# A bilinear block's contraction operands: one copy in DRAM, five replica slots and three product slots

## The chip, the cores and the metric

The kernel runs on one core of a Trainium2 chip. The metric is the device time of a whole launch in microseconds (us). The core has a matrix engine (TensorE, PE in the profile, with its weight loads as PEld), three engines for element-wise work (VectorE or DVE, ScalarE or ACT, GpSimd or POOL), SyncE (SP), which here only issues transfers, and sixteen DMA engines that all the queues share.

## The reference

The input is 16 images of 56 x 56 pixels with 128 channels in float32. Four blocks follow each other, each with a residual and a group normalization ahead of it: window attention, a triangle product, a Fourier operator, and a bilinear block. The change is in the last, which is, cut to what matters:

```python
xp = jax.nn.silu(x @ W1) @ W2                     # 160 channels: q (8 x 16), k (16), v (16)
q, k, v = ...                                     # each normalized over its 16 channels
K_H1 = conv(k, H1_w) + P1                         # per pixel 16 x 16
kernel = jnp.einsum('xnk,xkd->xnd', q, K_H1)      # contraction 1
feature = conv(v, H2_w)                           # per pixel 16 x 16
V_G = conv(v, G_w) + I                            # per pixel 16 x 16
feature = jnp.einsum('xvw,xvd->xwd', V_G, feature)
out = jnp.einsum('xnd,xvd->xvn', kernel, feature)
```

The convolutions are 3 x 7, one filter per pair of channels. The kernel regroups the last two contractions: kernel is contracted with the convolved features first (contraction 2), and the result with V_G (contraction 3). Every one of the three contracts, for each pixel, 8 rows of 16 numbers with a 16 x 16 matrix.

## The kernel before, in words

An image stays on chip as 128 channels x 3136 pixels. Images take one of two lanes in turn, and each lane has its own large scratch tile (the arena), its own small tiles, PSUM tiles and DRAM tiles, so two images are in work at a time. The program is traced image by image, block by block; what each engine gets, and in which order, is then laid out by the tile framework's planner, which plays the program forward with its own estimates of time (`schedule_with_timeline_sim=True`). The order on each engine and on each queue is fixed at build time: an engine or a queue whose next instruction waits does nothing else in the meantime.

The bilinear block (`_bilinear`) goes over an image in seven chunks of 448 pixels. `project` (L1291) makes the normalized input, the silu and the second product; its q part, 128 channels x 448 pixels in PSUM, goes to `kept`. Its k and v part is normalized and written to a zero-padded plane in DRAM (L1338, ScalarE's queue); `spread` (L1347, SyncE's queue) reads that back shifted by seven columns, which makes a convolution a matmul (`conv`, L1362 to L1369).

`kept` (L1284 to L1289) copies 128 x 448 numbers from PSUM to SBUF on ScalarE (L1287) and writes them to a tile in DRAM (L1288, ScalarE's queue; the tile is called dy in the profile). The DRAM tile is 128 x 3584: each row is written eight times side by side. `contract` (L1372) reads it back so that the 128 partitions hold 16 numbers, each for eight columns of the matrix: four reads of 448 KB each (L1381, SyncE's queue), each of two groups i, to a slot of `reps`, of which there are three. A product on VectorE (L1384) multiplies a replica with the matrix's two halves into a slot of `prods`, of which there are four. After two products (n = 0, then n = 1) TensorE sums them with a constant matrix in 16 matmuls of 32 columns (`together`, L364 and L367: the first goes ahead and the others are queued behind it). A contraction thus has four reads, four products and two groups of matmuls. Chunk by chunk there are three contractions, the first two of which end in `kept`, as the projection does: 3 x 7 x 16 = 336 writes, 1344 reads and 1344 products. The main loop takes, in one turn, contraction 3 of chunk q - 2, the projection of chunk q + 2, contraction 2 of chunk q - 1 and contraction 1 of chunk q.

All slots are reused in turn: a read waits until the product that last used its replica slot has ended, and a product until the matmuls that last read its product slot have ended. The arena has room for 9856 columns of both: 3 x 896 + 4 x 1792.

Of the kernel before, what the change touches and what calls it, by code (L numbers as in the profile page):

```python
# [36 lines left out]
F32 = mybir.dt.float32  # L37
# [5 lines left out]
P = 128  # L43
# [4 lines left out]
CH = 448  # L48
# [255 lines left out]
def tile_blocks(ctx: ExitStack, tc: tile.TileContext, ins, out, at, stages=(0, 1, 2, 3)):  # L304
    nc = tc.nc
# [5 lines left out]
    def pool(name, bufs, **kw):  # L311
        return ctx.enter_context(tc.tile_pool(name=name, bufs=bufs, **kw))
# [5 lines left out]
    dyp = [pool(f"dy{k}", 8, space=bass.MemoryType.DRAM) for k in range(2)]  # L318
# [5 lines left out]
    lane = [0]  # L324
    count = [0]

    def uid(s):
        count[0] += 1
        return f"{s}{count[0]}"
# [14 lines left out]
        return ps2[lane[0]].tile([P, 2, 512], F32, tag="ps2", name=uid("psd"))  # L344

    def dram():
        return dyp[lane[0]].tile([P, 8 * CH], F32, tag="dy", name=uid("dy"))

    def bc(ap, axis, n):

# [896 lines left out]
def _bilinear(env):  # L1247
    e = _Env(env)
    nc, mm, tt, ts, act, C, W, bc = e.nc, e.mm, e.tt, e.ts, e.act, e.C, e.W, e.bc
    reduce = nc.vector.tensor_reduce  # L1250
    NH, D = 8, 16
# [12 lines left out]
    def planes(t, start, dims):  # L1264

        return bass.AP(tensor=t.tensor, offset=t.offset + start, ap=[list(d) for d in dims])

    def run(b, xt):
        nm, rs = e.group_norm(xt)
        ar = e.arena()  # L1270
# [5 lines left out]
        staged = [ar[96:P, k * SPAN : (k + 1) * SPAN] for k in range(2)]  # L1276
        nc.gpsimd.memset(ar[96:P, 0 : 2 * SPAN], 0.0)
        zs = [ar[:, 3968 + k * 896 : 4864 + k * 896] for k in range(3)]
        reps = [ar[:, 6656 + k * 896 : 7552 + k * 896] for k in range(3)]
        prods = [ar[:, 9344 + k * 1792 : 11136 + k * 1792] for k in range(4)]  # L1280
        norms = ar[:TT, 16512:16792]
        count = [0, 0, 0]

        def kept(p):  # L1284

            t, d = e.w2(), e.dram()
            nc.scalar.copy(t[:, :CH], p[:, :CH])  # L1287
            nc.scalar.dma_start(out=d.rearrange("p (k t) -> p k t", k=8), in_=bc(t[:, :CH], 1, 8))  # L1288
            return d  # L1289

        def project(q):  # L1291
# [9 lines left out]
            mm(p[:, :CH], lhsT=W("l3w2a")[:, :P], rhs=ha[:, :CH], start=True, stop=False)  # L1301
            mm(p[:, :CH], lhsT=W("l3w2b")[:, :P], rhs=hb[:32, :CH], start=False, stop=True)
            dq = kept(p)
            sq = e.w2()
            act(sq[:, :CH], p[:, :CH], AF.Square)
# [66 lines left out]
        def contract(y, z):  # L1372

            acc = e.psb()
            yv = y.rearrange("(i n a) (k t) -> n (a k) i t", n=2, a=D, k=8)
            for n in range(2):
                done = []
                for two in (0, 2):
                    rep = reps[count[1] % 3].rearrange("p (i t) -> p i t", i=2)
                    count[1] += 1  # L1380
                    nc.sync.dma_start(out=rep, in_=yv[n][:, two : two + 2, :])  # L1381
                    t4 = prods[count[2] % 4].rearrange("p (i h t) -> p i h t", i=2, h=2)
                    count[2] += 1
                    tt(t4, bc(rep, 2, 2), bc(z, 1, 2), ALU.mult)  # L1384
                    done += [t4[:, 0], t4[:, 1]]
                e.together(
                    dict(
                        out=acc[32 * i : 32 * i + 32, :CH],
                        lhsT=C("red")[:, (2 * n + h) * 32 : (2 * n + h + 1) * 32],
                        rhs=done[i][:, h],  # L1390
                        start=n == 0 and h == 0,
                        stop=n == 1 and h == 1,
                    )
                    for h in range(2)
                    for i in (3, 0, 1, 2)
                )
            return acc

        def last(q, y, z):
            acc = contract(y, z)  # L1400
            y = e.w2()
            nc.scalar.copy(y[:, :CH], acc[:, :CH])
            p = e.psb()
            for a in range(4):
                nc.tensor.transpose(p[:TT, a * P : (a + 1) * P], y[:, a * TT : (a + 1) * TT], C("ident"))
            o = e.w2()
            tt(
                o[:TT, :].rearrange("p (a w n) -> p a n w", a=4, n=NH),
                p[:TT, :].rearrange("p (a n w) -> p a n w", a=4, n=NH),
                bc(norms[:, q * 40 : (q + 1) * 40].rearrange("p (a g) -> p a g", g=10)[:, :, :NH], 3, D),  # L1410
                ALU.mult,
            )
            p = e.psb()
            for a in range(4):
                c0 = q * CH + a * TT
                nc.tensor.transpose(p[:TT, a * P : (a + 1) * P], xt[:, c0 : c0 + TT], C("ident"))
            tt(o[:TT, :], p[:TT, :], o[:TT, :], ALU.add)
            nc.sync.dma_start(
                out=e.of[b, q * CH : (q + 1) * CH, :].rearrange("(a p) c -> p a c", p=TT),
                in_=o[:TT, :].rearrange("p (a c) -> p a c", a=4),  # L1420
            )
# [3 lines left out]
        for q in range(NCH + 2):  # L1425
            if 0 <= q - 2:
                last(q - 2, *feat.pop(q - 2))
            if q + 2 < NCH:
                queries[q + 2] = project(q + 2)
            if 0 <= q - 1 < NCH:  # L1430
                zf, zg = conv("l3wf", 1), conv("l3wg", 1)
            if q < NCH:
                spread(1, q)
            if 0 <= q - 1 < NCH:
                feat[q - 1] = kept(contract(kern.pop(q - 1), zf)), zg
            if q < NCH:
                zk = conv("l3wk", 0)
                if q + 1 < NCH:
                    spread(0, q + 1)
                kern[q] = kept(contract(queries.pop(q), zk))  # L1440
# [26 lines left out]
```

## Time and profile before

| what | value |
|---|---|
| median of 5 runs | 14956.74 us (14919.47 to 15004.44) |
| the profiled execution, and its span | 14989.26 us; 14987.2 us |
| granted TensorE clock, mean | 0.781 |
| PE, DVE, ACT, POOL busy | 78%, 63%, 25%, 9% |
| PE weight loads busy | 43% |
| moved by DMA | 2106.93 MB, mean 141 GB/s |
| q1 (SyncE's queue) | 560,000 packets, 823.94 MB, 17.7% of sixteen engines |
| q10 (ScalarE's queue) | 365,712 packets, 639.44 MB, 12.1% |
| q0 (GpSimd's queue, the Fourier block's table reads) | 165,120 packets, 629.61 MB, 15.7% |
| replica writes (dy<-w, L1288) | 336, of 1792 KB each |
| replica reads (arena<-dy, L1381) | 1344, of 448 KB each |
| products (L1384) | 1344, mean 2018 ns |
| a copy of `kept` on ScalarE (L1287) | 336, mean 532 ns |

The profile is of one execution. A row of its cost groups has the line, the engine, the operation, what it writes and reads, how often, the busy time in us, the mean of one in ns, and the idle time of the engine just ahead of it, with what ended most of that. Lines L364 and L367 are helpers, shared by several blocks; the contraction's matmuls there are those with psb<-arena,cst and 128*32. Time that an engine's queue spends waiting is counted for the queue (SPq is SyncE's). KB of a transfer are those that the instruction moves.

### The profile page before, as it was taken

What the parts mean: (1) busy time and instruction counts of PE and PEld (TensorE: products, weight loads), DVE (VectorE), ACT (ScalarE), POOL (GpSimd) and SP (SyncE); (2) the same over time, 40 slices, a digit from 0 to 9 for tenths busy, and PEclk for the clock granted to TensorE, in tenths of its full rate; (3) what the DMA queues carried; (4) which work ended last, traced back from release to release, by engine and by line L of the source; (5) the groups of instructions that cost most, each with busy time, mean ns of one, the idle gap of its engine ahead of it and who ended that gap; (6) DMA issues with size and microseconds to landing.
All of it is one profiled execution on the core that took longest, in us unless ns stands there. A gap on an engine that the chain in (4) does not pass through costs nothing. (4 is left out here: it accounts for less than half of the span.)

```text
span 14987.2 us, 218307 instructions
## 1 busy us (share of the span) xinstructions
PE 11644.3 (78%) x91360; PEld 6410.9 (43%) x91360; DVE 9494.1 (63%) x13537; ACT 3724.7 (25%) x6236; POOL 1326.9 (9%) x2554
## 2 busy tenths in 40 slices
PE   7788687876888778877778777887778877778665
PEld 5454354533544334533345344453434534345342
DVE  6765766667665666656675666747667575665645
ACT  3222231222322223212223122231322313223111
POOL 0120001100011000110010100201002010020010
PEclk9877888778877788777886778868787777886767
DMA  1336704475045751274631736418264272642636
GB/s 31 99 113 229 259 5 117 129 258 192 11 111 166 235 177 40 72 216 154 215 90 40 224 120 209 127 46 241 95 207 112 75 226 83 210 107 77 203 88 217
DMA packets 1091813, 2106.93 MB, mean 141 GB/s; under 512 B 98320, under 2 KB 974096, under 8 KB 1089680
## 3 DMA queue, kind: packets, MB, share of 16 engines
q1 hardware_dynamic: 560000, 823.94, 17.7%
q0 software_dynamic: 165120, 629.61, 15.7%
q10 hardware_dynamic: 365712, 639.44, 12.1%
q8 instruction: 722, 11.83, 0.3%
q14 instruction: 259, 2.12, 0.0%
HBM read 1412.72 MB, written 667.03 MB: 139 GB/s over the span
## 5 line engine op out<-in xcount | busy, mean ns | idle before, releaser
L1384 DVE TENSOR_TENSOR arena<-arena 128x1792 f32<-128x1792 f32 x1344 | 2669.8, 2018 | 1285.9 <-DMA arena<-dy 997.8
L364 PE MATMUL psb<-arena,cst 128*32 128x448 f32 (+1 forms) x1728 | 1111.6, 735 | 1205.8 <-DVE arena L1384 1103.4
L367 PE MATMUL psb<-arena,cst 128*32 128x448 f32 (+1 forms) x10368 | 2031.9, 705 | 1.8 <-ACT arena L995 1.7
L1173 DVE TENSOR_TENSOR arena<-arena 112x1344 f32<-112x1344 f32 x1024 | 1569.2, 1554 | 453.9 <-DMA arena<-table 429.6
L367 PE MATMUL psd<-arena 112*64 112x224 f32 (+1 forms) x6144 | 1477.8, 472 | 0.0
L1171 POOL DMA_DIRECT2D arena<-table x2048 | 1055.2, 518 | 3726.0 <-PE psd L367 1002.5
L364 PE MATMUL psd<-arena 112*64 112x448 f32 x2048 | 1130.2, 639 | 99.0 <-DVE arena L1173 94.3
L364 PEld LDWEIGHTS psb<-arena,cst 128*32 128x32 f32 (+1 forms) x1728 | 205.2, 155 | 1603.9 <-DVE arena L1384 1084.8
L367 PEld LDWEIGHTS psd<-arena 112*64 112x64 f32 x6144 | 619.1, 156 | 591.5 <-issue 580.4
L367 PEld LDWEIGHTS psb<-arena,cst 128*32 128x32 f32 (+1 forms) x10368 | 580.2, 143 | 650.8 <-issue 578.7
L662 PE MATMUL psd<-wgt,arena 128*64 128x128 f32 x7168 | 582.4, 313 | 120.7 <-DVE arena L674 93.4
L1067 DVE TENSOR_TENSOR arena<-w,coef 128x1792 f32<-128x1792 f32 x256 | 507.4, 2020 | 195.4 <-PE psb L367 184.3
L662 PEld LDWEIGHTS psd<-wgt,arena 128*64 128x64 f32 x7168 | 493.2, 157 | 297.6 <-issue 219.6
L1369 ACT COPY arena<-psd 128x896 f32<-128x896 f32 x336 | 304.4, 906 | 1238.7 <-DVE arena L1384 843.3
L887 PEld LDWEIGHTS psb<-cst,arena 128*64 128x64 f32 x10752 | 509.5, 198 | 145.4 <-issue 70.3
L887 PE MATMUL psb<-cst,arena 128*64 128x32 f32 (+1 forms) x10752 | 526.1, 272 | 57.8 <-ACT arena L853 40.9
L367 PE MATMUL psd<-arena,wgt 85*32 85x448 f32 x2688 | 511.3, 635 | 24.8 <-DMA arena<-padded 24.7
L367 PE MATMUL psb<-arena 128*64 128x448 f32 x1792 | 511.4, 648 | 0.0
L1287 ACT COPY w<-psb 128x448 f32<-128x448 f32 x336 | 178.8, 532 | 1337.6 <-PE psb L367 1046.7
L364 PE MATMUL psd<-arena,wgt 85*32 85x448 f32 x896 | 453.6, 629 | 64.9 <-DMA arena<-padded 43.8
L585 PE MATMUL psb<-cst,arena 128*49 128x128 f32 x2048 | 357.6, 329 | 167.5 <-DVE arena L580 56.4
L1196 PE MATMUL psb<-cst,w 128*112 128x56 f32 x1024 | 185.9, 347 | 329.1 <-DVE w L1193 328.1
(290 smaller groups left out, 19435.4 us busy)
## 6 DMA issues: line engine op xcount, KB each, us to landing
arena<-table POOLq DMA_DIRECT2D x2048, 294.0 KB, 9.2
dy<-w ACTq DMA_DIRECT2D x336, 1792.0 KB
arena<-dy SPq DMA_DIRECT2D x1344, 448.0 KB
arena<-padded SPq DMA_DIRECT2D x896, 162.8 KB
w<-x SPq DMA_DIRECT2D x112, 224.0 KB
out<-w SPq DMA_DIRECT2D x112, 224.0 KB
padded<-arena ACTq DMA_DIRECT2D x336, 62.0 KB
arena<-arena POOLq DMA_DIRECT2D x16, 784.0 KB, 10.4
```

The source lines that it names most:

```text
L364: done = mm(**first)
L367: mm(**kw)
L585: nc.tensor.transpose(p[:WIN, i * P : (i + 1) * P], s3[:, 4 * g + i, :], C("ident"))
L662: mm(p[half : half + 64, i // 4, i % 4 * P : (i % 4 + 1) * P], lhsT=xh[:, c0 : c0 + 64], rhs=W(w).rearrange("p (k c) -> p k c", c=64)[:, : ...
L887: mm(p[64 * c : 64 * c + 64, i * nl : (i + 1) * nl], lhsT=src[:, t * T : t * T + 64], rhs=fc[:, c], start=True, stop=True)
L1067: tt(t4, bc(ys[c][:, l0 : l0 + 4, :], 1, 8), bc(coef[:, c, h0 : h0 + 8, l0 : l0 + 4], 3, T), ALU.mult,)
L1171: nc.gpsimd.dma_start(out=t[hh * T : (hh + 1) * T, :], in_=bc(tflat[q, two, hh], 0, T))
L1173: tt(t4, bc(x3[:, :, s], 1, 2), t4, ALU.mult)
L1196: mm(p[:TT, l * T : (l + 1) * T], lhsT=o[:, l * TT : (l + 1) * TT], rhs=C("unpair"), start=True, stop=True)
L1287: nc.scalar.copy(t[:, :CH], p[:, :CH])
L1369: nc.scalar.copy(z, p[:, :, :CH])
L1384: tt(t4, bc(rep, 2, 2), bc(z, 1, 2), ALU.mult)
```

## The change

The DRAM tile shrinks from 128 x 3584 to 128 x 448, and `kept` writes each row once. The 128 rows stand in SBUF in the order (i, n, a) with i of 4, n of 2 and a of 16; in DRAM they are now ordered (n, a, i), so that the groups i of one (n, a) lie side by side. `contract`'s read takes two neighbouring groups as one run of 896 numbers and repeats it for eight partitions, by a step of 0 in the source; before, it read two runs of 448 for each partition, each from its own copy. The bytes that land in SBUF are the same. The replica slots become five and the product slots three; the columns that both take in the arena stay 9856 (5 x 896 + 3 x 1792).

```diff
     def dram():
-        return dyp[lane[0]].tile([P, 8 * CH], F32, tag="dy", name=uid("dy"))
+        return dyp[lane[0]].tile([P, CH], F32, tag="dy", name=uid("dy"))
...
-        reps = [ar[:, 6656 + k * 896 : 7552 + k * 896] for k in range(3)]
-        prods = [ar[:, 9344 + k * 1792 : 11136 + k * 1792] for k in range(4)]
+        reps = [ar[:, 6656 + k * 896 : 7552 + k * 896] for k in range(5)]
+        prods = [ar[:, 11136 + k * 1792 : 12928 + k * 1792] for k in range(3)]
...
             nc.scalar.copy(t[:, :CH], p[:, :CH])
-            nc.scalar.dma_start(out=d.rearrange("p (k t) -> p k t", k=8), in_=bc(t[:, :CH], 1, 8))
+            nc.scalar.dma_start(out=planes(d, 0, ((CH, 4), (4 * CH, 32), (1, CH))), in_=t[:, :CH])
             return d
...
             acc = e.psb()
-            yv = y.rearrange("(i n a) (k t) -> n (a k) i t", n=2, a=D, k=8)
             for n in range(2):
                 done = []
                 for two in (0, 2):
-                    rep = reps[count[1] % 3].rearrange("p (i t) -> p i t", i=2)
+                    rep = reps[count[1] % 5]
                     count[1] += 1
-                    nc.sync.dma_start(out=rep, in_=yv[n][:, two : two + 2, :])
-                    t4 = prods[count[2] % 4].rearrange("p (i h t) -> p i h t", i=2, h=2)
+                    nc.sync.dma_start(out=rep, in_=planes(y, (n * D * 4 + two) * CH, ((4 * CH, D), (0, 8), (1, 2 * CH))))
+                    rep = rep.rearrange("p (i t) -> p i t", i=2)
+                    t4 = prods[count[2] % 3].rearrange("p (i h t) -> p i h t", i=2, h=2)
                     count[2] += 1
                     tt(t4, bc(rep, 2, 2), bc(z, 1, 2), ALU.mult)
                     done += [t4[:, 0], t4[:, 1]]
```

`planes(t, start, dims)` is a helper that was there before: it returns a view of a DRAM tile from an element on, with the (step, count) pairs given.

## The prediction

> **What bounds the kernel now.** I read the page's busy shares first, then the cost groups, then who waited for whom, on the engines and on SyncE's queue, then the chain of waits in one stretch, then the DMA queues.
>
> ```profile
> PE 11644.3 (78%) x91360; PEld 6410.9 (43%) x91360; DVE 9494.1 (63%) x13537; ACT 3724.7 (25%) x6236; POOL 1326.9 (9%) x2554
> L1384 DVE TENSOR_TENSOR arena<-arena 128x1792 f32<-128x1792 f32 x1344 | 2669.8, 2018 | 1285.9 <-DMA arena<-dy 997.8
> ```
>
> No engine is full. TensorE (PE) is the most loaded, at a mean granted clock of 0.781. The dearest single group is the contraction's product on VectorE (DVE), L1384: 2.018 us each, and 1285.9 us of idle time just ahead of it, 997.8 of that until a replica read (arena<-dy) landed.
>
> ```profile
> PE psb L364 <- DVE arena L1384: 1103.4, 295, 21.9
> DVE arena L1384 <- DMA arena<-dy: 997.8, 289, 19.5
> SPq L1381 <- DMA dy<-w: 1747.5, 177, 313.6
> SPq L1381 <- DVE arena L1384: 1664.4, 651, 26.5
> ```
>
> The columns are total us, times, longest. TensorE in its turn stands 1103.4 us for products. The two queue lines say what holds the reads back: the landing of the replica write (177 times), and a replica slot still in use by a product (651 times).
>
> ```profile
> 14720.24 1.52 PE psb L1331 x7
> ...
> 14726.39 9.65 DMA dy<-w
> 14736.09 5.10 DMA arena<-dy
> 14741.31 2.04 DVE arena L1384
> 14743.36 4.00 DMA arena<-dy
> 14747.49 2.04 DVE arena L1384
> 14749.57 0.96 PE psb L364
> ```
>
> This is the chain of waits (start, length) in the last image, which runs alone: write 9.65 us, first read 5.10, one product, then another 4.00 us for the fourth read, which had no slot until the first product ended. In the stretch 11420 to 14987 us, all that the chain covers, dy<-w holds 5.0% and arena<-dy 8.9%: 0.139 x 3567 = 496 us.
>
> ```profile
> q1 hardware_dynamic: 65536, 98.32, 48.1%
> q10 hardware_dynamic: 42288, 73.86, 32.7%
> ```
>
> These are the DMA queues (packets, MB, share of 16 engines) at 1195 to 1820 us, where two images are in this block together: the sixteen engines are 81% busy, and q10, ScalarE's, a third of everything, is almost only the eightfold write.
>
> [...]all queues share the same engines. It shows at 14729.27, where a read was issued, and its packets ran from 14734.34 to 14736.46, after those of a write at 14727.95 to 14735.60. [...]The trace has both rates: a contraction group of 16 matmuls takes 1.71 us or 3.2 us.
>
> **The change, part by part.**
>
> *Write.* 336 writes go from 1024 packets to 128, of the same 1792 B. Median packet: 74 ns. Now 64 packets on each engine, 64 x 80 (mean) = 5.1 us; measured, first to last packet, 4.8 at best, median 6.8. The new destination's slowest dimension is 4, [...]32 x 74 = 2.4 us, stretched as today (6.8/5.1) 3.2 us. Saved about 4 us a write; the ends are 3.6 and, if all sixteen engines take part, 6. Engine time: 336 x 1024 x 80/16 = 1720 us becomes 215. ScalarE's queue issues a write in 0.52 us as before, or less. The rest relieves reads that queue behind a write, worth about 1 us each.
>
> *Read.* 1344 reads go from 256 packets of 1792 B to 128 of 3584 B. Medians of 27, 74 and 81 ns for 512, 1792 and 1984 B give 37 ns per KB: 140 ns for 3584 B, so 8 x 140 = 1.12 us against 16 x 74 = 1.18. The eight equal reads of one row cost nothing extra, I say: the padded reads already fetch each row seven times, shifted by one, at 81 ns for 1984 B. Bounds: 0 to +0.5 us each. Its source has one more dimension: SyncE takes 0.36 us to issue a read now and 0.76 for the three-dimensional padded read. I charge +0.3 us once in a contraction, 100 us in all, half on the path: 50.
>
> *Five replica slots.* Read j waits for product j-5, not j-3, so a contraction's four reads go out together. From the trace's products, sorted by place: of the 997.8 us, products one to three hold 663 (184 waits) and product four 334 (105 waits, nearly all the slot). Each of the 184 shortened by at most 5 us (4 of write, 1 of congestion): 480. Product four: 334. Together 814 us.
>
> *Three product slots.* Product j waits for the matmuls of product j-3, not j-4. In pairs of two, this moves odd products from the group two back to the group just before: product four can't start until the group of the first two has ended. Product three (2.02 us) covers a group of 1.71 us, not one of 3.2: 1.2 us of wait then. If TensorE is busy with the other image, group one ends later still: now it ends 1.3 us (median) and 6.7 us (upper quartile) after product three. Laid on the present order of TensorE (end of group one + 2.13 us against start of group two), 157 of 336 second groups would start later, 283 us in all. While VectorE waits, everything behind it stands: the other image's products, L1173 among them, and so their matmuls. Measured on VectorE in the present order this wait would come to 1694 us; the planner sees the slot, and puts other work there or not. I take the 283.
>
> *Sum.* 814 - 283 - 50 = 481 us. The images share the engines, and part of it only uncovers the other image's chain; yet on the chain these transfers weigh more (496 us in 3567) than the waits that they cause on VectorE there (325.9). I take three quarters, 360. [...]if a fifth of 672 groups goes from 3.2 to 1.71 us, 134 x 1.5 = 200, half of it on the path, 100. Total 460 of the profiled execution's 14989.3 (span 14987.2): 14,529. The runs' median is 32 us lower: 14,497; with some give for the planner's new order, **14,520**.
>
> **The rivals.**
> - *Hidden.* TensorE's queue, 78% busy and in order, ends the waits anyway; what VectorE gains is spent behind the other image's matmuls. For: the pieces of the chain at TensorE outweigh DMA. Against: 1103 us of TensorE waiting for L1384. Then some 30 us: 14,930.
> - *Product slots decide (slower).* The place is product four. If nearly half of the 1694 us stays, 45% or 760 us, against a realized gain of 0.75 x 814 - 50 = 560, and none from the clock: 14,957 + 200 = 15,160. It decides once that wait is over about 560 us, a third of 1694, or 1.7 us a contraction. For: a group under the slow clock alone costs 1.2. Against: 156 of the 336 first groups start within 0.3 us of their product.
> - *Transfers don't get shorter (slower).* Eight packets for one address, or four engines, run slow: 2 us more on each of the 336 first reads, 672 us. Then 14,957 + 672 + 283 + 50 - 814 = 15,150. Padded's repeated reads speak against.
> - *More.* The 814 us count in full; the clock, and shorter table reads of the other image's Fourier block (L1173 waits 429.6 us for them on the same engines), pay for the slots: 14,957 - 814 = 14,140.
>
> **How the numbers follow.** Forecast 0.55 (its own range 14,300 to 14,800); more 0.12; hidden 0.13; product slots 0.15; transfers slow 0.05. Hidden lies around the bound of 0.3% (45 us, about what a measurement can tell): 0.04 faster, 0.07 same, 0.02 slower. Faster 0.55 + 0.12 + 0.04 = 0.71; same 0.07; slower 0.15 + 0.05 + 0.02 = 0.22. The range from 14,130 to 15,120 leaves out half of "more" and most of the two slower cases, some 0.2.
>
> **What would show it.** Right: dy<-w falls to 224 KB and q10 from 12.1% to under 3%; 43,008 large packets there, 1344 completions for them[...]. SyncE's wait for L1384 falls from 1664 to under 400 us; L1384's wait for arena<-dy falls from 998 to under 350 us. Its wait for TensorE (PE psb L367, 161.1 us now) rises to 300 to 600; over 900 means the slot rival. The clock is 0.79 or more. Wrong: packets of 3584 B well over 160 ns; an unchanged wait for arena<-dy; or both waits down and TensorE's wait moved to another line.

## The result: no change, and where the profile differs

The changed kernel takes 14984.14 us (median of 36 runs), the kernel before beside it 14973.77: a ratio of 1.0005, with a 95% interval of 0.9994 to 1.0016. The forecast was 14,520. The profiled execution spans 14970.8 us at a granted clock of 0.783.

The page's busy shares, the costliest group on VectorE and the DMA queues, after (columns as before):

```profile
PE 11661.9 (78%) x91360; PEld 6398.0 (43%) x91360; DVE 9498.8 (63%) x13537; ACT 3751.3 (25%) x6261; POOL 1333.0 (9%) x2554
...
q1 hardware_dynamic: 387968, 823.94, 21.4%
...
q10 hardware_dynamic: 60624, 99.93, 2.4%
...
L1384 DVE TENSOR_TENSOR arena<-arena 128x1792 f32<-128x1792 f32 x1344 | 2674.1, 2020 | 1339.4 <-DMA arena<-dy 878.1
```

ScalarE's queue is almost empty: 12.1% of sixteen engines' time became 2.4%. SyncE's queue moves the same bytes in fewer packets and yet takes more time: 17.7% became 21.4%. VectorE's idle time ahead of the products is no smaller, 1339.4 us after 1285.9.

Who waited for whom on the engines (total, times, longest):

```profile
DVE arena L1384 <- DMA arena<-dy: 878.1, 246, 24.7
...
PE psb L364 <- DVE arena L1384: 733.8, 286, 23.8
...
DVE arena L1173 <- DMA arena<-table: 567.5, 506, 14.8
...
DVE arena L1384 <- PE psb L367: 372.2, 199, 9.9
```

Before the change, what VectorE's L1384 waited for (a part), and the line of the table reads:

```profile
  DMA arena<-dy: 997.8, 289
  PE psb L367: 161.1, 62
...
DVE arena L1173 <- DMA arena<-table: 429.6, 427, 11.7
```

The wait for a replica is down only from 997.8 to 878.1; the wait for TensorE is up from 161.1 to 372.2, as three product slots in place of four would have it; and the Fourier block of the other image waits longer for its table reads, 567.5 us after 429.6, though a quarter of all bytes has gone from the DMA engines.

The same on SyncE's queue, whose read is now at L1380:

```profile
SPq L1380 <- DMA dy<-w: 2541.2, 236, 326.8
...
SPq L1380 <- DVE arena L1384: 650.2, 325, 18.2
```

Replica slots hold the reads back far less (1664.4 us before); the landing of the write does so more (1747.5 before), although the write has an eighth of the bytes that it had. (The experiments show that both come with the slots.) The chain of waits shows the two links in the last image, start and length:

```profile
14662.91 5.58 DMA dy<-w
14668.55 4.05 DMA arena<-dy
...
14674.67 2.04 DVE arena L1384
```

This write is 5.58 us where the forecast showed one of 9.65, its first read 4.05 where 5.10 stood. They are among the shorter ones: in the last image the chain has seven writes before and seven after, with a median of 9.36 and 8.56 us, and twelve and eleven reads, with 4.09 and 5.77. Over all that the chain covers (11440 us to the end) the write has 5.5% and the read 6.0%, after 5.0% and 8.9%.

Sorted by the product's place in its contraction, as in the forecast (VectorE's products counted off in fours), its waits moved like this (us):

| place | replica read, before | after | TensorE, before | after |
|---|---|---|---|---|
| first product | 522.8 (117 times) | 786.2 (174) | 139.2 | 12.5 |
| second and third | 140.6 | 64.0 | 19.2 | 34.7 |
| fourth | 334.3 (105) | 28.0 (8) | 2.7 | 325.0 (162) |

And the packet and transfer records, median unless said otherwise:

| | before | after |
|---|---|---|
| packet of a read, median (mean) | 74 ns (91) for 1792 B | 231 ns (228) for 3584 B |
| time that the packets of all reads took, on each of 16 engines | 1957 us | 2449 us |
| a read's issue on SyncE | 0.36 us | 0.55 us |
| a read, first to last packet | 2.11 us | 2.20 us |
| a write, first to last packet | 6.79 us | 3.76 us |
| four-byte packets of a write on ScalarE's queue | 16 (of 10,768) | 4 (of 6736) |
| packets of one write under way at once, the number that holds longest | 16 (in 248 of 336 writes) | 4 (in 249) |
| from the write's issue to the first read's issue, shortest | 6.53 us | 5.09 us |
| from the write's issue to where VectorE has come to the first product | 20.2 us | 12.5 us |
| from the write's issue to the start of that product | 21.0 us | 15.0 us |

The write's two counts, 16 before and 4 after, are read here as sixteen and four DMA engines. The packets of all queues together stand at 14 to 16 at once for 4.7 of the 8.3 ms in which any is under way before, and at 18 or more for 0.5, which fits sixteen engines that all queues share.

The last two rows pair each write with the contraction that reads it. VectorE comes to the first product 7.7 us sooner, and the data come sooner by less than that where VectorE waits for them. In part that is the order laid out at build time: where a contraction reads the result of another, the other instructions that stand between the two on VectorE take 14.0 us before and 10.4 after (median of 224 such pairs).

### The profile page after: what moved, and what is told of

Read it like the earlier page. It is cut to its first block, busy times and chain, and to the rows that moved or that the text cites. A ratio compares the mean times of both kernels' runs of the same rounds, so it can differ in the third digit from the quotient of the medians.

```text
span 14970.8 us, 218471 instructions
## 1 busy us (share of the span) xinstructions
PE 11661.9 (78%) x91360; PEld 6398.0 (43%) x91360; DVE 9498.8 (63%) x13537; ACT 3751.3 (25%) x6261; POOL 1333.0 (9%) x2554
## 3 DMA queue, kind: packets, MB, share of 16 engines
q1 hardware_dynamic: 387968, 823.94, 21.4%
q10 hardware_dynamic: 60624, 99.93, 2.4%
## 5 line engine op out<-in xcount | busy, mean ns | idle before, releaser
L1384 DVE TENSOR_TENSOR arena<-arena 128x1792 f32<-128x1792 f32 x1344 | 2674.1, 2020 | 1339.4 <-DMA arena<-dy 878.1
L367 PE MATMUL psb<-arena,cst 128*32 128x448 f32 (+1 forms) x10368 | 2014.1, 691 | 3.5 <-DVE arena L1216 1.8
L1173 DVE TENSOR_TENSOR arena<-arena 112x1344 f32<-112x1344 f32 x1024 | 1573.3, 1555 | 588.9 <-DMA arena<-table 567.5
L364 PE MATMUL psb<-arena,cst 128*32 128x448 f32 (+1 forms) x1728 | 1095.6, 724 | 878.0 <-DVE arena L1384 733.8
L367 PEld LDWEIGHTS psd<-arena 112*64 112x64 f32 x6144 | 628.5, 156 | 596.5 <-issue 582.7
L367 PEld LDWEIGHTS psb<-arena,cst 128*32 128x32 f32 (+1 forms) x10368 | 553.9, 140 | 635.7 <-issue 592.6
L364 PEld LDWEIGHTS psb<-arena,cst 128*32 128x32 f32 (+1 forms) x1728 | 195.0, 153 | 1267.5 <-DVE arena L1384 776.0
L364 PEld LDWEIGHTS psd<-arena 112*64 112x64 f32 x2048 | 287.8, 157 | 364.3 <-DVE arena L1173 228.6
L1362 PE MATMUL psd<-arena,wgt 85*128 85x448 f32 x896 | 423.1, 620 | 17.6 <-ACT arena L1369 11.2
## 6 DMA issues: line engine op xcount, KB each, us to landing
arena<-arena POOLq DMA_DIRECT2D x16, 784.0 KB, 10.4
```

The costliest lines, as they stand in the source:

```text
L364: done = mm(**first)
L367: mm(**kw)
L1173: tt(t4, bc(x3[:, :, s], 1, 2), t4, ALU.mult)
L1362: mm(p[:, h, :CH], lhsT=wt[:, g * P : (g + 1) * P], rhs=rows[:, g], start=g == 2 * h, stop=g == 2 * h + 1)
```

## The experiments

Times are medians; each ratio is to the kernel before, run beside it on the same chip, with its 95% interval. Diffs are against the changed kernel unless said otherwise. The medians of the kernel before, beside the experiments, lie between 14,979.5 and 14,984.5 us, so that the times of different experiments can be compared too. Three theories were tried against each other: that the *slots* gave back what the transfers gained; that the *reads* of one address by eight partitions are slow; that the *write's four engines* keep it long. Beside them stands that the *plan*, the order laid out at build time, comes nearer by as much as the transfers get shorter.

The packets of ScalarE's queue, without those of 1792 B and more, give the engines of other writes in the same way: 64,656 packets in e4 and 107,664 in e10 leave 10,768 of four bytes, 16 a write, and 60,624 in e12 leave 6736, 4 a write. For e5, e6, e8, e9 and e11 the number of engines is not shown; where an expectation names one for these, it was an assumption of mine.

### Slots and transfers apart

```diff
# e1: the new transfers, the old slots
-        reps = [ar[:, 6656 + k * 896 : 7552 + k * 896] for k in range(5)]
-        prods = [ar[:, 11136 + k * 1792 : 12928 + k * 1792] for k in range(3)]
+        reps = [ar[:, 6656 + k * 896 : 7552 + k * 896] for k in range(3)]
+        prods = [ar[:, 9344 + k * 1792 : 11136 + k * 1792] for k in range(4)]
# e2: the kernel before with the reverse of this
# n3, against the kernel before: three product slots, and still three replica slots
-        prods = [ar[:, 9344 + k * 1792 : 11136 + k * 1792] for k in range(4)]
+        prods = [ar[:, 11136 + k * 1792 : 12928 + k * 1792] for k in range(3)]
```

(The counters' moduli follow.) Expected of e1:

> The new transfers with the old slots (three replicas, four products). Theory 'slots' (three product slots gave back what the transfers gained): L1384's wait for TensorE falls from 372 us to under 100, and the time lies 1% or more under the kernel before, 14,700 to 14,830 us. Theory 'plan' (what the transfers save is given back because the planner puts the product sooner behind a cheaper write, so that the waits stay): within 0.3% of before, L1384's wait for arena<-dy still 800 us or more. Theory 'reads' (eight reads of one address are slow): packets of 3584 B stay at about 230 ns here, and the time is as the changed kernel's or longer, since three replica slots hide less of it.

Measured: 15124.84 us, 1.0097 (1.0067 to 1.0127). Expected of e2:

> The old transfers with the new slots (five replicas, three products). Theory 'slots': slower than before by 1% or more, 15,100 to 15,250 us, with L1384 waiting 300 us or more for TensorE. Theory 'plan': within 0.3%, because a fourth read that goes out early repays the wait for the matmuls: L1384's wait for arena<-dy 650 to 750 us, for TensorE about 350.

Measured: 14803.53 us, 0.9879 (0.9853 to 0.9905). The theories "slots" and "plan" miss the time in both runs; of those named for e1 only "reads" has the time right, though its packets of 3584 B took 201 ns there and not 230. The new slots gain 1.2% with the old transfers, and the new transfers lose: 0.97% with the old slots, and with the new ones what is between 0.9879 and 1.0005. The result of no change is a sum of two changes.

What SyncE's queue waited for in e2, with the old eightfold write:

```profile
SPq L1381 <- DMA dy<-w: 2433.4, 211, 329.6
...
SPq L1381 <- DVE arena L1384: 785.4, 350, 23.1
```

That is close to the 2541.2 and 650.2 us of the changed kernel; in e1 they are 1779.2 and 1294.4. A read that finds a slot free waits for the write instead, so the longer wait for the write's landing says nothing against the new write. VectorE's waits for a replica, by place, tell the same:

| | first product | fourth |
|---|---|---|
| before | 522.8 us | 334.3 us |
| e1, the new transfers | 527.4 | 488.8 |
| e2, the new slots | 701.8 | 23.8 |
| both | 786.2 | 28.0 |

The slots take the wait away from the fourth product, and at the first products it grows; VectorE's idle time ahead of the products is 1294 us in e2, after 1286. The loss of e1, 142 us, is about what it waits longer at the fourth product, whose read still has to wait for a slot: 154 us. (Another order alone, n2 below, moved the two columns to 482.4 and 404.6, so only the larger differences count.) Both parts bring the order nearer: the 14.0 us of work on VectorE between two contractions are 11.3 in e1 and 12.2 in e2, and VectorE comes to the first product 13.3 and 17.6 us (median) behind the write's issue where it was 20.2. Expected of n3:

> The kernel before with three product slots and still three replica slots: the price of the product slot alone. By the forecast's step 283 us or 1.9% slower, 15,200 to 15,300 us. If a product that waits for its matmuls costs nothing because its replica was not there any sooner, within 0.4% of before, and the 1.2% that the new slots gained with the old transfers come from the two replica slots.

Measured: 14967.27 us, 0.9984 (0.9971 to 0.9996). Who waited for whom in n3, and then in e2:

```profile
DVE arena L1384 <- DMA arena<-dy: 941.3, 274, 14.9
PE psb L364 <- DVE arena L1384: 906.1, 285, 18.3
...
DVE arena L1384 <- PE psb L367: 309.0, 154, 8.8
```

```profile
PE psb L364 <- DVE arena L1384: 916.4, 296, 22.6
...
DVE arena L1384 <- DMA arena<-dy: 841.2, 229, 19.8
...
DVE arena L1384 <- PE psb L367: 343.1, 191, 10.2
```

With one product slot less VectorE waits 148 us more for TensorE, and the kernel is no slower; TensorE's own wait for products even falls, from 1103.4 to 906.1. The two replica slots are then worth 0.9879 / 0.9984, about 1%. (All this is with the old transfers. A changed kernel with four product slots was not run.)

### The reads

```diff
# e5: eight copies again, but with pairs side by side; four writes of 32 rows
-            nc.scalar.dma_start(out=planes(d, 0, ((CH, 4), (4 * CH, 32), (1, CH))), in_=t[:, :CH])
+            for i in range(4):
+                nc.scalar.dma_start(out=planes(d, i * CH, ((32 * CH, 32), (4 * CH, 8), (1, CH))), in_=bc(t[32 * i : 32 * i + 32, :CH], 1, 8))
...
-planes(y, (n * D * 4 + two) * CH, ((4 * CH, D), (0, 8), (1, 2 * CH)))
+planes(y, (n * D * 32 + two) * CH, ((4 * CH, P), (1, 2 * CH)))
# e7: one copy, each partition at an address of its own
-planes(y, (n * D * 4 + two) * CH, ((4 * CH, D), (0, 8), (1, 2 * CH)))
+planes(y, (n * 4 + two) * CH, ((384, P), (1, 2 * CH)))
```

Expected of e5 (its DRAM tile is the eightfold one again):

> The changed kernel's reads of 3584 B and its slots, but from eight copies in DRAM as before the change, so that no address is read twice[...]. Theory 'reads': packets of 3584 B fall from 231 ns (median) to 140 to 160 ns. If they stay above 200 ns the size or the crowd of reads in flight is the cause, not the repeated address. Time: the write is again long, so 15,000 to 15,200 us by 'reads' and 'slots', within 0.3% of before by 'plan'.

Measured: 15143.41 us, 1.0103 (1.0068 to 1.0139). The packets of 3584 B take 140 ns (median; mean 174) where they took 231 (228): it is the repeated address, not the size. The write is 9.7 us long here, so the time says nothing on the reads. Expected of e7:

> The changed kernel, but each of the 128 partitions reads 896 numbers from an address of its own (384 numbers apart) and not eight from one; the packets keep their number and size, the write its four engines. The contractions thus work on other numbers than the reference's. Theory 'reads' (the repeated address costs, and it is on the path): packets of 3584 B at 140 ns (median) where they took 231, a read first to last 1.3 to 1.6 us where it took 2.2, and 14,700 to 14,880 us. Theory 'write engines' (the four-engine write alone keeps the gain away): packets shorter in the same way, but the time within 0.5% of before, 14,900 to 15,040.

Measured: 14598.45 us, 0.9741 (0.9713 to 0.9769), packets again 140 ns (mean 171). The time is below the range of either theory, 2.6% or 386 us under the changed kernel.

Two things differ in it, and no run parts them for these reads: the repeated address, and the issue of a read on SyncE, whose source has one dimension less and which takes 0.38 us where it took 0.55 (median; 228 us less over all reads). Nor is a read shorter by eight packets of 91 ns. From first to last packet it takes 2.00 us where it took 2.20, and not the 1.3 to 1.6 expected. The reads that ran with no other packet beside them took 1.88 us in e7 (25 reads), 1.91 in the changed kernel (8) and 1.94 before (144). What fell is the time that the packets of all reads take on each engine, 1839 us after 2449. So the repeat costs little or nothing where a read is alone, and shows where many reads share the engines. VectorE's waits for the replica and for the other image's table, 878.1 and 567.5 us in the changed kernel, are lower too:

```profile
DVE arena L1384 <- DMA arena<-dy: 708.5, 201, 24.0
...
DVE arena L1173 <- DMA arena<-table: 449.4, 467, 13.6
```

e2 and e7 have the same slots and reads of nearly the same cost (1.95 and 2.00 us from first to last packet, 0.41 and 0.38 us to issue, 1875 and 1839 us of packets on each engine), so that what differs is in the main the write. That splits the result of no change in three: the slots take 179 us off (before to e2), the new write 205 (e2 to e7), and the new reads, with their repeat and their longer issue, put 386 on (e7 to the changed kernel).

### The write's engines

```diff
# e6: four writes of 32 rows in place of the one
+            for i in range(4):
+                nc.scalar.dma_start(out=planes(d, i * CH, ((4 * CH, 32), (1, CH))), in_=t[32 * i : 32 * i + 32, :CH])
# e8: two writes of 64 rows in place of the one
+            for i in (0, 2):
+                nc.scalar.dma_start(out=planes(d, i * CH, ((CH, 2), (4 * CH, 32), (1, CH))), in_=t[32 * i : 32 * i + 64, :CH])
# e9: e6 with the old slots
```

Expected of e6:

> The changed kernel with its write cut in four transfers of 32 rows[...]: first to last packet 1.0 to 1.8 us where four engines take 3.8, for 1.2 us more on ScalarE's queue. If the write's length is on the path, 336 x 2 = 670 us of chain are at stake and the time falls by 150 to 350 us (14,640 to 14,830); by 'plan' it stays within 0.3%, with L1384 waiting for arena<-dy 750 us or more.

Measured: 14415.03 us, 0.9621 (0.9594 to 0.9648), more than expected, though the write took 2.9 us from first to last packet and not 1.0 to 1.8. Expected of e8:

> The changed kernel with its write cut in two transfers of 64 rows whose slowest dimension is 2[...]: first to last packet 6.5 to 7.5 us where four engines take 3.8 and sixteen 2.9. Theory 'write engines': a dose and its response, 3 us more on 336 writes, 15,300 to 15,600 us. Theory 'reads': the write's length is not what counts, 14,900 to 15,080 us.

Measured: 15030.06 us, 1.0029 (1.0015 to 1.0044). The write takes 6.3 us, and the time is where "reads" put it. The dose did not work as I had thought: the first read needs only groups 0 and 1, so it waits for the first of the two writes alone, half of the 128 packets, and goes out 4.7 us behind the issue at the soonest, little sooner than in the changed kernel (5.1). The wait of the second product, which needs the second write, rises from 43 to 212 us. For the same reason e6 mixes two things: a shorter write (2.9 us after 3.76), and a first read that waits for half of the rows. Expected of e9:

> Four write transfers on sixteen engines, single copy, with the old slots (three replicas, four products). If slots and transfers add up as in the runs so far (new slots 1.2% faster with the old transfers, 0.9% with the changed ones), this is 1% slower than the same with new slots: 14,520 to 14,620 us. If the slots matter only where the write is long, within 0.3% of 14,415.

Measured: 14856.13 us, 0.9922 (0.9894 to 0.995), in neither range: slots and transfers don't just add up. With the shorter write the new slots are worth 3% (14,856 to 14,415).

A pair without that mixture keeps the rows in their order in SBUF, so that one write of 128 rows is contiguous; a replica is filled by two reads. The second kernel of the pair only sets the four groups one row apart, which makes the slowest dimension of the write 4 (its DRAM tile has four rows more):

```diff
# e4
-            nc.scalar.dma_start(out=planes(d, 0, ((CH, 4), (4 * CH, 32), (1, CH))), in_=t[:, :CH])
+            nc.scalar.dma_start(out=d, in_=t[:, :CH])
...
-                    nc.sync.dma_start(out=rep, in_=planes(y, (n * D * 4 + two) * CH, ((4 * CH, D), (0, 8), (1, 2 * CH))))
                     rep = rep.rearrange("p (i t) -> p i t", i=2)
+                    for k in range(2):
+                        nc.sync.dma_start(out=rep[:, k], in_=planes(y, ((two + k) * 32 + n * D) * CH, ((CH, D), (0, 8), (1, CH))))
# e12, against e4
-            nc.scalar.dma_start(out=d, in_=t[:, :CH])
+            nc.scalar.dma_start(out=planes(d, 0, ((33 * CH, 4), (CH, 32), (1, CH))), in_=t[:, :CH])
...
-planes(y, ((two + k) * 32 + n * D) * CH, ((CH, D), (0, 8), (1, CH)))
+planes(y, ((two + k) * 33 + n * D) * CH, ((CH, D), (0, 8), (1, CH)))
```

Expected of e4:

> One copy in the order in which the rows stand in SBUF: one write of 128 rows with a slowest dimension of 128[...], first to last 0.6 to 1.0 us; each replica is read by two transfers of 128 packets of 1792 B, again eight times from one address. Theory 'write engines': 14,350 to 14,550 us, as with four 16-engine writes. Theory 'reads': the 2688 reads cost more than before; packets of 1792 B over 100 ns (74 before the change) and 14,600 us or more.

Measured: 14364.08 us, 0.958 (0.9553 to 0.9608), with 16 four-byte packets a write. Expected of e12:

> The kernel with rows in their natural order and one write (14,364 us), its four groups of 32 rows now 33 rows apart in DRAM, so that the write's slowest dimension is 4[...]; nothing else differs but the order that the planner makes of it. Theory 'write engines': first to last packet 3.5 us or more where sixteen engines took 0.75 to 1.7, the first read goes out 5 us behind the write and not 2, and the time rises by 2.5 to 4%, to 14,720 to 14,940 us. If the natural order's gain came from its reads, it stays within 0.5% of 14,364.

Measured: 14930.61 us, 0.9965 (0.995 to 0.9981), 3.9% or 567 us above e4, with 4 four-byte packets a write. Who waited for whom, in e4 and then in e12 (L1385 is the product there):

```profile
PE psb L364 <- DVE arena L1385: 589.5, 270, 14.9
...
DVE arena L1385 <- DMA arena<-dy: 399.6, 166, 24.5
```

```profile
DVE arena L1385 <- DMA arena<-dy: 840.7, 235, 21.5
...
PE psb L364 <- DVE arena L1385: 672.6, 270, 18.0
```

The wait for a replica doubles, and its growth, 441 us, is as large as most of the 567. The first read goes out 1.94 us behind the write's issue at the soonest in e4, with sixteen engines by that count, and 5.10 in e12, with four. The order hardly differs: VectorE comes to the first product 9.6 and 10.6 us (median) behind the write's issue, with 10.3 and 10.1 us of work between two contractions. One more thing differs, ScalarE's issue of the write: 0.34 and 0.52 us, 62 us over all writes.

### How often one address is read

Two and four copies in the natural order, each read four times and twice, and one copy with addresses of their own:

```diff
# against e4, c = 2 (e10) or 4 (e11); the DRAM tile is c * CH wide
-            nc.scalar.dma_start(out=d, in_=t[:, :CH])
+            nc.scalar.dma_start(out=d.rearrange("p (k t) -> p k t", k=c), in_=bc(t[:, :CH], 1, c))
...
-planes(y, ((two + k) * 32 + n * D) * CH, ((CH, D), (0, 8), (1, CH)))
+planes(y, ((two + k) * 32 + n * D) * c * CH, ((CH, c * D), (0, 8 // c), (1, CH)))
# e13, against e4, in place of the same line
+planes(y, ((two + k) * 2 + n) * CH, ((384, P), (1, CH)))
```

> The kernel with rows in their natural order (16-engine write), with each partition reading 448 numbers from an address of its own, 384 numbers apart; the contractions work on other numbers than the reference's. Theory 'reads': packets of 1792 B fall from 99 ns (median) to 74, a read's first to last by 0.3 to 0.4 us, and the time by 0.5 to 2.5%, to 14,000 to 14,290 us. If the repeated address cost time only beside the four-engine write, within 0.3% of 14,364.

> Natural order with two copies in DRAM, so that an address is read four times instead of eight; the write is 256 packets on sixteen engines. Theory 'reads': packets of 1792 B in the reads at 80 to 92 ns (99 with one copy, 74 with eight), and the time 0.2 to 1% under 14,364 us, as the write grows by only 0.6 us.

> Natural order with four copies, an address read twice; the write is 512 packets on sixteen engines, some 2.5 us. Theory 'reads': packets at 74 to 80 ns. Time: what the reads gain the write takes, within 0.5% of 14,364 us; if the number of reads of an address doesn't count, slower than with one copy by 0.5 to 1.5%.

| | reads of an address | packet of a read, median (mean) | write, first to last | time | ratio |
|---|---|---|---|---|---|
| e4 | 8 | 99 ns (104) | 1.7 us | 14364.08 us | 0.958 (0.9553 to 0.9608) |
| e10 | 4 | 74 (90) | 2.2 | 14254.67 | 0.9529 (0.9502 to 0.9555) |
| e11 | 2 | 74 (91) | 3.9 | 14481.43 | 0.968 (0.9656 to 0.9703) |
| e13 | none alike | 74 (92) | 1.5 | 14112.07 | 0.9436 (0.9411 to 0.9462) |

With four reads of an address the packets are already as fast as with none alike. From there more copies only lengthen the write. The cleanest price of the repeat is e10 against e4: 109 us less, though the write is longer, at the same issue time of a read (0.59 us). The 252 us of e13 also hold a shorter issue (0.42 us, 472 us less over 2688 reads), and its reads are not shorter from first to last packet, as expected, but 1.13 us after 1.05. The time of e11, 0.8% above e4, is where it was expected if the repeat did not count: its write of 3.9 us takes back more than the reads gain.

Two copies make the fastest of these kernels that computes the reference (e7 and e13 work on other numbers), 4.7% below the kernel before. The new slots count in it too:

> Two copies, natural order, with the old slots (three replicas, four products). With short transfers the new slots were worth 3.0% beside the four 16-engine writes; by that 14,600 to 14,720 us here, where the new slots gave 14,255. If what the slots are worth is only the planner's order, within 1% of 14,255.

Measured with the old slots: 14525.55 us, 0.9688 (0.9663 to 0.9713), a little under the range expected, so the new ones are worth 1.9% there.

### What another order alone is worth

Every edit makes the planner lay out another order. One short instruction more for each image, on VectorE, was added to the changed kernel (n1) and to the one before (n2):

```diff
+        nc.vector.memset(ar[:, 16800:17152], 0.0)
```

> The changed kernel with one more short memset on VectorE for each image (about 0.2 us each, 3 us in all), which makes the planner lay out another order from there on. If orders of this kind differ by little, within 0.4% of the changed kernel's 14,984 us; if differences of 1% come from the order alone, it is off by 0.5 to 1.5% one way or the other, and the effects of the slots (1%) can't be told from that, while those of the write's engines (3.8%) can.

> The kernel before with the same short memset. Within 0.4% of before if the order alone matters little, 0.5 to 1.5% off if it matters.

Measured: 1.002 (1.0005 to 1.0035) for n1, that is 0.2% above the changed kernel, and 0.9969 (0.9954 to 0.9983) for n2. In these two trials another order was worth 0.2 and 0.3%. As far as two trials can tell, the effects of about 1% and more above stand out of that; n3's 0.16% doesn't, and means none.

## Why the prediction was wrong, step by step

- **"The eight equal reads of one row cost nothing extra" failed.** The working expected 140 ns for a packet of 3584 B; it took 231, and took 140 where each partition had an address of its own (e5, e7). Of the bounds given, 0 to 0.5 us a read, I took 0 and charged 50 us for the issue alone. The packets of all reads took 2449 us on each engine after 1957, 0.37 us a read, and by e7 the new reads cost 386 us of time. How much of that is the repeat and how much the issue stays open; e10 gives 109 us, with a longer write, for the repeat of half-size reads. The issue itself was charged about right: 0.3 us once in a contraction, 100 us in all, against 0.36 to 0.55 us a read, 120 in all. The padded reads, from which I argued, read a row seven times but each time from another address, one number on; that is not the same case.
- **The forecast of 14,520 is near e7's 14,598, and that is luck.** e7 is the change without the repeat, but the other terms missed in both directions: the slots, put at 334 - 283 = 51 us, gained 179; the shorter write, put at 480, gained 205; and VectorE still waits 708.5 us for replicas there, where under 350 was expected.
- **The write: the four engines were right, the saving was mis-sized.** That four would carry it was an estimate of mine, which nothing before the change showed for this write. It came out so: ScalarE's queue shows 6736 four-byte packets after 10,768, which is 4 a write in place of 16 (1344 in all, as forecast), and 249 of the 336 writes have four packets under way at once for longest, where 248 had sixteen. But I took 32 x 74 ns, stretched to 3.2 us, and a saving of 4. Writes with no other packet beside them took 3.6 us, some 110 ns a packet, after 4.98, and the median of all is 3.76 after 6.79: 3.0 us saved at the median, and only 1.4 where a write runs alone (6.53 to 5.09 us until the read can go out). Another 567 us came with 4 four-byte packets a write in place of 16, by e12 against e4, whose reads are of half the size.
- **"Each of the 184 shortened by at most 5 us: 480" failed.** The first product's wait grew from 522.8 to 786.2 us. I subtracted from waits as if each stood by itself. By e2 most of the growth comes with the slots: they take the wait from the fourth product, and the first one's is 701.8 us with the old transfers. By e1 the new transfers alone leave the first product's wait where it was (527.4): the write is shorter, but VectorE also comes to the product sooner. That the planner's lower estimate of the cheaper write lays out this nearer order is not shown.
- **Five replica slots: right on the wait, too high on its worth.** The fourth product's wait fell from 334.3 to 28.0, and SyncE's wait for the products from 1664.4 to 650.2 (under 400 was expected). Their worth in time, about 1%, or 150 us, is less than three quarters of 334.
- **Three product slots: the wait was right, its price wrong.** VectorE waits 325.0 us at the fourth product, against 283 by my working, but by n3 the kernel before pays nothing for such a wait. That TensorE works on the group meanwhile would be a reason; it is argued, not shown. The slower rival, which hung on this wait, falls with it.
- **Hidden.** Its time came near (14,930), but not its reason: e7's 14,598 and e13's 14,112 show that what the transfers cost is on the path. Nothing was hidden; gains and a loss of the same size were added.
- **The clock** stayed at 0.783, after 0.781. It was higher where the kernel was faster: 0.798 in e4, 0.802 in e10. That shorter waits raise it, for which the forecast took 100 us, was an assumption of mine and is not shown.

Of the signs that the forecast named for being wrong, packets of 3584 B well over 160 ns came true, and the wait for arena<-dy, 878.1 us after 997.8, came close to unchanged.

## What to carry to other kernels

A transfer's cost is not its bytes: look at how many DMA engines carry it (the write of e12, with a slowest dimension of 4, showed four where that of e4, with 128, showed sixteen, and took 567 us more), and at how many readers fetch one address (with eight a packet of 1792 B took 99 ns in e4, with four 74 in e10). What a transfer saves can't be subtracted from the waits one by one: here one place's wait fell and another's grew, and an order laid out anew moves the consumer too. When a change has several parts and no effect, run the parts apart before looking for a reason why nothing happened.

## What the runs showed of the hardware that I had not expected

Eight reads of one address, 128 packets in all, took 231 ns a packet of 3584 B (changed kernel) and 99 ns one of 1792 B (e4), where addresses of their own took 140 (e7) and 74 (e13). Four reads of one address took 74 ns (e10), no more than two (e11). The padded reads, seven times over almost the same bytes but each one number further, took 81 ns for 1984 B before and after. The slow packets did not make a lone read longer: with no other packet beside it a read took 1.91 us with the repeat, 1.88 without, though only eight such reads are in the trace of the changed kernel. Why eight of the same are slow and four are not, nor seven shifted ones, stays open.
